# Two fp4 feed-forward stages: when the third group of rows is normalised, scaled and rounded

## The chip, the cores and the metric

The kernel runs on one core of a Trainium2 chip. Its engines are TensorE (PE; its weight loads are shown as PEld), VectorE (DVE), ScalarE (ACT), GpSimd (POOL) and SyncE (SP), which issues most of the transfers. The metric is the time of one execution in device microseconds; 2608.18 us is the median of the three runs before the change (2606.8 to 2610.64). Each profile is of one execution and has a time of its own.

## The reference, cut to what matters

The reference is a chain of six residual blocks on `x`, 8192 rows of 256 numbers (8 x 1024 x 256): an fp4 feed-forward block, an attention with decaying state, the same fp4 block again, a ternary feed-forward block, an attention with memories, the ternary block again. The change touches the two fp4 blocks:

```python
def fp4_quant_dequant(x):            # along the last dim, blocks of 16
    scale = max(|block|) / 6         # at least 1e-12
    idx = searchsorted(_MID, |x / scale|)
    return _GRID[idx] * sign(x) * scale   # grid 0 .5 1 1.5 2 3 4 6
def fp4_linear(x, w):
    return einsum('bsk,nk->bsn', fp4_quant_dequant(x), fp4_quant_dequant(w))

n = layernorm(x)                          # per row of 256
h = silu(fp4_linear(n, w_gate)) * fp4_linear(n, w_up)    # 704 wide
x = x + 0.5 * fp4_linear(h, w_down)
...
x = x + decay_attention(layernorm(x)); then the fp4 block again
```

So a row is normalised, cut into 16 blocks, each divided by its scale and rounded to the fp4 grid; the product goes through the gate and is quantised a second time, in 44 blocks, ahead of the last product.

## The kernel before, in words

All of `x` lies in SBUF as 16 groups (`NG`) of 4 tiles (`G`), a tile being 128 rows. `ffn_fp4` is called twice: `ffn_fp4(True, "decay")` is the first stage, which prepares weights on the way, and `ffn_fp4(False, "ternary")` the second; `attn_decay("fp4")` lies between them. Each call runs a loop over `i`, one pass per tile (64 tiles and a short tail), with `g, j = divmod(i, G)`. A helper `pin` fixes the order of the instructions on each engine to the order in which the code issues them, transfers on SP's queue included.

One pass for tile `i` does this. PE makes the two halves of the gate and the up product (`products`, L835; `pg` has one buffer, `pu` two). ACT takes the silu (`sg`, L846), DVE multiplies (`h`, L848). Between the halves ACT takes the magnitudes of the tile before (L795) and DVE rounds it to a bf16 grid `gd` (`round_grid`, L858, two instructions). After the second half DVE finds the block scales of this tile's `h` (`scale`, L783 to L787), POOL divides by them (L791), and ACT copies the scales (L790) for PE to turn in the next pass (`scales_turned`, L863).

The scales of the tile before go through `spread`: ACT copies them (`sct`, L869), SP writes them to DRAM (`sd`, L871), turns the grid by a transposing transfer (`gt`, L884) and reads the scales back, spread over the partitions, into `ht` (L876). Two passes later POOL multiplies grid and scales (`multiplied`, L899; called by `scaled_turn`), and PE makes the last product one pass after that (`down`, L932), which DVE adds to `x` (L941). In the first stage `down` begins at tile 5.

The rows that later tiles need come the same way. For a group `t` of 2 or more, in halves of two tiles: ACT normalises into `xn` (`ln.normalize`, L317 subtracts the mean, L325 multiplies), DVE and POOL scale it, ACT takes magnitudes (`mgx`) and DVE rounds to a bf16 grid, which lies in the same bytes as the first tile of that half of `xn`. The pass after that SP turns this grid (`gtx`, L1048, one buffer) and the scales, which went with that tile's own through `spread`, come back into `xt` (L876, second call). A pass later POOL multiplies them. There is one `xn` buffer for all groups, so the normalising of the next group into a half must wait for the turn of the grid there.

Before the change the times of these steps follow one rule for every group `t`:

| step | half 0 | half 1 |
|---|---|---|
| normalise | 4t-7 | 4t-5 |
| scale | 4t-6 | 4t-4 |
| round | 4t-5 | 4t-3 |
| turn the grid | 4t-4 | 4t-2 |
| multiply | 4t-3 | 4t-1 |

For the third group (`t` = 2) half 0 is thus normalised in tile 1, scaled in 2, rounded in 3, turned in 4 and multiplied in 5; group `t` = 3 is normalised into half 0 in tile 5. The groups 0 and 1 are made ahead of the loop or by PE's transposes in tile 3.

The statistics come from `statistics(sizes, dues)`: groups are taken together by `sizes`, and each lot is spread evenly over the tiles up to the due tile of its first group. A lot is `bn_stats` and `bn_aggr` on each tile (L235, L236) and then four terms for all its rows at once (L248 to L264: a seed and three Newton steps of a reciprocal square root, on DVE). `ln.advance(i - 1, 1)` issues the terms, in tile `i` ahead of the normalising, and `ln.advance(i, 0)` the tile statistics, at the end of tile `i`. The lots that are due at tile 0 are done before the stage: for the second stage by `begin("fp4", ...)`, which spreads them over 12 passes near the end of `attn_decay`, and ends with normalising group 0.

In the first stage `prepared(i)` adds to the tiles 1 to 4 the quantising of the last weights (`prep_down_scale`, L378 to L384; `prep_down`, L391 to L395), and tile 5 turns them on PE (`prep_down_turn`, L641), two PSUM buffers that ACT empties (`wd`, L645). The load of `raw_w` (L962) then goes on SP's queue.

Of the kernel before, what the change touches and what calls it, by code (L numbers as in the profile page):

```python
# [18 lines left out]
P = 128  # L19
D = 256  # L20
# [19 lines left out]
def macaron_kernel(  # L40
# [227 lines left out]
    def statistics(sizes, dues):  # L268
# [75 lines left out]

    NT = NG * G
    PLANS = {
        "start": ((2, 1, 1, 2, 4, 4, 2), [max(0, G * (g - 2) + 1) for g in range(NG)]),
        "fp4": ((2, 1, 1, 2, 4, 4, 2), [max(0, G * (g - 2) + 1) for g in range(NG)]),

        "decay": ((2, 2, 4, 4, 4), [max(0, G * g - 5) for g in range(NG)]),  # L350
        "ternary": ((2, 2, 4, 4, 4), [max(0, g - 1) for g in range(NG)]),
# [393 lines left out]
    def ffn_fp4(prepare, after):  # L745
        with ExitStack() as st:
# [164 lines left out]
            def turn(i):  # L911
                h, _ = hs.pop(i)
                ht = hp.tile([P, NC, P], F32, tag="ht", name="ht", bufs=HT_BUFS)
                for c0, c1 in ((0, 4), (4, 5), (5, 6)):
                    kn = DCH[c0][1]
                    pa = ps_t.tile([P, 4, P], F32, tag="pt", name="pt")
                    for c in range(c0, c1):
                        k0 = DCH[c][0]
                        pin(
                            nc.tensor.transpose(pa[:kn, c - c0, :], h[:, k0 : k0 + kn], ident)  # L920
                        )
                    pin(nc.scalar.copy(ht[:kn, c0:c1, :], pa[:kn, : c1 - c0, :]))
                hts[i] = (ht, DCH[-1][1])
# [61 lines left out]
            sc1 = fp4_scale(v1, lnp, nc.gpsimd, pin)  # L985
            xts[1] = (xn1,)

            xn = None
            downs = 0

# [3 lines left out]
            for i in range(NT + 3):  # L994
                g, j = divmod(i, G)
                h = hp.tile([P, NI], F32, tag="h", name="h") if i < NT else None

                to = (i + 7) // G
                to_do = to < NG and i > 0
                half = 0 if j in (1, 2, 3) else 1  # L1000
                if i == 0 and not prepare:
                    xts[0], copied = turn_products(xts[0])
                    copied()
                pts = None
                for q in range(2):
                    if i < NT:
                        pg = ps_h.tile([P, NHALF], F32, tag="pg", name="pg", bufs=1)
                        pu = ps_h.tile([P, NHALF], F32, tag="pu", name="pu")
                        products(i, q, 0, pg)
                        if q == 1 and i == 3:  # L1010
                            xts[1], copied = turn_products(xts[1][0])
                        if prepare and late_weights and q == 1:
                            late_weights.pop()(ps_t)
                        if q == 1 and by_dma(i - 1):
                            pts = scales_turned(i - 1)
                        products(i, q, 1, pu)
                        gated(h, q, pg, pu)
                    if q == 0:
                        while copies and i < NT:
                            copies.pop(0)()  # L1020
                    elif i == 3:
                        copied()

                    if 0 < i < NT and q == 0:
                        magnitudes(hs[i - 1][0], qp[:, 0:NI])
                        if by_dma(i - 1):
                            round_grid(hs[i - 1][0], qp[:, 0:NI], gd[:, :NI])
                    if i == NT - 1:
                        if q == 1:
                            round_(*hs[i - 1], qp[:, 0:NI])  # L1030

                        part = h[:, q * NHALF : (q + 1) * NHALF]
                        at = NI + q * NHALF // 8
                        mul = nc.vector if q else nc.gpsimd
                        halves.append((part, scale(part, hp, at, mul)))
                    if i == NT:
                        copies.pop(0)()
                        part, sc = halves.pop(0)
                        mg = ps_h.tile([P, NHALF], F32, tag="pu", name="mg")
                        magnitudes(part, mg)  # L1040
                        round_(part, sc, mg, nc.vector if q else nc.gpsimd)
                if pts is not None:
                    spread(i - 1, pts)
                for to_, half_ in list(xgrids):
                    gx, at = xgrids[to_, half_]
                    if at == i - 1:
                        gt = lnp.tile([P, G, P], BF16, tag="gtx", name="gtx", bufs=1)
                        pin(nc.sync.dma_start_transpose(out=gt, in_=gx))  # L1048
                        xgrids[to_, half_] = (gt, at)
                if i == 0:  # L1050
                    mgs = [qp[:, 0 : 2 * D], ps_t.tile([P, 2 * D], F32, tag="pt", name="mg1")]
                    for n in range(2):
                        magnitudes(v1[:, 2 * D * n : 2 * D * (n + 1)], mgs[n])
                if 0 < i < NT:

                    ln.advance(i - 1, 1)
                if to_do and j % 2 == 1:
                    if j == 1:
                        to_n, tiles = to, (0, 1)
                        if xn is None:  # L1060
                            xn = xn_pool.tile([P, G, D], F32, tag="xn", name="xn")
                    else:
                        to_n, tiles = (i + 5) // G, (2, 3)
                    if to_n < NG:
                        for n in tiles:
                            ln.normalize(xn, to_n, n, pin)
                if by_dma(i - 3):
                    scaled_turn(i - 3)
                if NT - 2 <= i - 2 < NT:
                    turn(i - 2)  # L1070
                for key in list(xgrids):
                    gt, at = xgrids[key]
                    if at == i - 2:
                        xgrids.pop(key)
                        to_m, half_m = key
                        multiplied(xts[to_m][:, G * half_m : G * half_m + G, :], gt)
                if i < NT:
                    own = scales[i % 2] if by_dma(i) else None
                    if own is not None:
                        scale(h, hp, NI, sc=own[:, : NI // 16])  # L1080
                        hs[i] = (h, own)
                    else:
                        hs[i] = (h, scale(h, hp, NI) if i < NT - 1 else None)

                    if j % 2 == 0 and i > 1:
                        to_s, half_s = ((i + 6) // G, 0) if j == 2 else ((i + 4) // G, 1)
                        if 1 < to_s < NG:
                            scale(
                                x_part(half_s), lnp, NI + 88,
                                sc=own[:, NC * 8 : NC * 8 + 2 * D // 16],  # L1090
                            )
                            xhalf[i] = (to_s, half_s)
                    if j % 2 == 1 and i > 1:
                        to_r, half_r = ((i + 5) // G, 0) if j == 3 else ((i + 3) // G, 1)
                        if 1 < to_r < NG:
                            v = x_part(half_r)
                            mg = ps_t.tile([P, 2 * D], F32, tag="pt", name="mgx")
                            magnitudes(v, mg)
                            gx = v.bitcast(BF16)[:, 0 : 2 * D]
                            round_grid(v, mg, gx)  # L1100
                            xgrids[to_r, half_r] = (gx, i)
                    if i == 0:
                        nb = 2 * D // 16
                        for n in range(2):
                            round_(
                                v1[:, 2 * D * n : 2 * D * (n + 1)],
                                sc1[:, nb * n : nb * (n + 1)], mgs[n],
                            )
                    ln.advance(i, 0)
                    if NT - 18 <= i < NT - 2:  # L1110
                        begin(after, NT - 2 - i)
                if prepare and i == DOWN:
                    prep_down_turn(ps_t, "pt")
                if i >= DOWN or not prepare:
                    first = downs
                    while downs <= (i - 4 if i < NT else i - 3) and downs < first + 2:
                        down(downs, *((ps_t, "pt") if downs > first else ()))
                        downs += 1
                if prepare:
                    prepared(i)  # L1120
# [964 lines left out]
```

## Time and profile before

| | us |
|---|---|
| median of the runs | 2608.18 |
| profiled execution | 2604.35 |
| its span | 2602.6 |
| first fp4 stage (34 to 563 of the span) | 529, PE busy 498.22 |
| decay attention (563 to 1004) | 441, PE busy 435.46 |
| second fp4 stage (1004 to 1500) | 496, PE busy 484.29 |
| rest (1500 to 2602) | 1102, PE busy 1080.9 |

The borders between the stages are read off the timeline by eye. In the timeline a line gives the start in microseconds, the duration, the engine (SPq is SP's queue), the line of the kernel, the operation, what it writes and reads, and in square brackets how long the engine stood idle before it and what released it. On the timeline tile 1 of the second stage starts near 1010 and its tile 5 near 1045.

### The profile page before, as it was taken

The numbers are of one execution on the slowest core, as the hardware profiler recorded it, in microseconds if no ns is written. First come the engines' busy times: TensorE is split into PE (matmuls) and PEld (weight loads), VectorE is DVE, ScalarE is ACT, GpSimd is POOL, SyncE is SP. The second block draws the span as 40 slices with busy tenths as digits, with TensorE's granted clock in tenths as the row PEclk, the third lists the DMA queues.
The fourth block names the chain that finished last, engine by engine and source line by source line (L and its number), as shares of the span: only waits on it lengthen the run. The fifth ranks groups of instructions, "written<-read, shape, count | busy, mean of one in ns | idle before, by whom it ended". The sixth has DMA issues, their size and how long they took to land.

```text
span 2602.6 us, 52695 instructions
## 1 busy us (share of the span) xinstructions
PE 2504.2 (96%) x20426; PEld 1864.2 (72%) x20426; DVE 2107.9 (81%) x5040; ACT 1235.8 (47%) x2785; POOL 902.6 (35%) x895
## 2 busy tenths in 40 slices
PE   4899999999999998999999999999999999999999
PEld 2566776766666665677777789995677767678998
DVE  7899999858777678998889789657888888879864
ACT  5344444433433333444444366665555555437664
POOL 4555555521100102555555400004555555540000
PEclk9899999999999999999999999999999999999999
DMA  7455565510000001556555300000000000000001
GB/s 218 99 111 120 119 114 112 110 32 2 2 2 2 2 2 29 113 117 116 115 114 118 81 1 1 1 1 1 2 2 2 2 2 2 2 2 25 33 33 42
DMA packets 197883, 130.32 MB, mean 50 GB/s; under 512 B 137824, under 2 KB 173696, under 8 KB 197632
## 3 DMA queue, kind: packets, MB, share of 16 engines
q1 hardware_dynamic: 196688, 125.75, 22.3%
q8 instruction: 161, 2.64, 0.4%
q0 software_dynamic: 240, 0.54, 0.1%
q14 instruction: 90, 0.74, 0.1%
q10 hardware_dynamic: 704, 0.66, 0.1%
HBM read 78.67 MB, written 16.52 MB: 37 GB/s over the span
## 4 chain that ended last, share of the span: by engine, by line
PE 80%; DVE 11%; ACT 3%; DMA 3%; issue 2%; POOL 1%; SPq 1%; DVEq 0%; POOLq 0%; ACTq 0%
PE po L932 10%; PE po L1207 9%; PE pg L835 9%; PE ph L1180 9%; PE pu L835 8%; PE sc L1250 5%; PE py L1334 5%; PE pq L1348 4%; PE pkv L1348 4%; PE pk L1348 4%; PE po L1348 4%; PE py L1316 2%; PE pmo L1765 2%; DVE at L1259 1%; DMA gtx<-xn 1%
## 5 line engine op out<-in xcount | busy, mean ns | idle before, releaser
L835 PE MATMUL pg<-wgu,xt 128*128 128x352 f32 x1024 | 350.0, 465 | 13.4 <-ACT sg L846 13.1
L932 PE MATMUL po<-wd,ht 128*128 128x256 f32 x1536 | 356.0, 382 | 2.3 <-DVE x L941 1.8
L835 PE MATMUL pu<-wgu,xt 128*128 128x352 f32 x1024 | 348.9, 464 | 2.1 <-DVE h L848 1.9
L932 PEld LDWEIGHTS po<-wd,ht 128*128 128x128 f32 x1536 | 291.7, 191 | 66.0 <-issue 4.1
L791 POOL TENSOR_TENSOR h<-h,q_rs 128x704 f32<-128x704 f32 (+1 forms) x128 | 176.3, 1378 | 419.9 <-DVE q_rs L787 419.9
L846 ACT ACTIVATE sg<-pg 128x352 f32<-128x352 f32 x256 | 117.8, 460 | 399.3 <-PE pg L835 394.0
L835 PEld LDWEIGHTS pg<-wgu,xt 128*128 128x128 f32 x1024 | 194.9, 192 | 108.5 <-ACT sg L846 21.1
L835 PEld LDWEIGHTS pu<-wgu,xt 128*128 128x128 f32 x1024 | 187.1, 193 | 103.3 <-issue 14.7
L1207 PE MATMUL po<-w,hl 128*128 128x256 f32 x1024 | 243.9, 280 | 1.4 <-DVE hl L1191 1.2
L1207 PE MATMUL po<-w,hh 128*128 128x256 f32 x1024 | 243.4, 280 | 0.0
L1881 POOL TENSOR_TENSOR mo<-mo 128x256 f32<-128x256 f32 x192 | 164.3, 856 | 195.0 <-DVE mo L1778 186.5
L899 POOL TENSOR_TENSOR ht<-gt,ht 128x768 f32<-128x768 bf16 x124 | 206.4, 1664 | 0.0
L1180 PE MATMUL ph<-xh,w 128*128 128x512 f32 x512 | 204.4, 401 | 1.4 <-ACT hf L1188 0.6
L1180 PE MATMUL ph<-xl,w 128*128 128x512 f32 x512 | 202.2, 396 | 0.0
L1191 DVE TENSOR_TENSOR hl<-hf,hh 128x512 fp32r<-128x512 f32 x256 | 168.2, 683 | 39.6 <-ACT hh L1189 36.1
L1207 PEld LDWEIGHTS po<-w,hl 128*128 128x128 f32 x1024 | 192.1, 188 | 4.5 <-DVE hl L1191 2.5
L1207 PEld LDWEIGHTS po<-w,hh 128*128 128x128 f32 x1024 | 192.0, 188 | 2.6 <-DVE x L1215 0.3
L848 DVE TENSOR_TENSOR h<-sg,pu 128x352 f32<-128x352 f32 x256 | 131.6, 514 | 60.0 <-PE pu L835 53.1
L1188 ACT ACTIVATE hf<-ph,b1c 128x512 f32<-128x512 f32 x256 | 168.3, 696 | 18.5 <-PE ph L1180 16.1
L1259 DVE TENSOR_TENSOR at<-sc,dec 128x512 f32<-128x512 f32 x256 | 158.5, 681 | 16.6 <-PE sc L1250 16.5
L1259 DVE TENSOR_TENSOR at<-sc,tri 128x512 f32<-128x512 f32 x256 | 164.6, 678 | 0.4 <-PE sc L1250 0.4
L1189 ACT CAST hh<-hf 128x512 fp32r<-128x512 f32 x256 | 149.2, 628 | 17.0 <-PE po L1207 15.2
(276 smaller groups left out, 5304.0 us busy)
## 6 DMA issues: line engine op xcount, KB each, us to landing
ht<-sd SPq DMA_DIRECT2D x124, 384.0 KB
xt<-sd SPq DMA_DIRECT2D x56, 256.0 KB
sd<-sct SPq DMA_DIRECT2D x124, 64.0 KB
x<-in_x SPq DMA_DIRECT2D x15, 512.0 KB
out<-x SPq DMA_DIRECT2D x15, 512.0 KB
raw_w<-in_w_t SPq DMA_DIRECT2D x2, 1024.0 KB
gt<-gd SPq DMA_TRANSPOSE x124
gtx<-xn SPq DMA_TRANSPOSE x56
```

The costliest lines, as they stand in the source:

```text
L791: pin(mul.tensor_tensor(vb, vb, rs[:, :, None].to_broadcast([P, nb, 16]), ALU.mult))
L835: nc.tensor.matmul(ps, lhsT=xts[g][:, 2 * j + k, :], rhs=wgu[:, k, (2 * q + of_up) * NHALF : (2 * q + of_up + 1) * NHALF], start=(k == 0), ...
L899: nc.gpsimd.tensor_tensor(wide.rearrange("p c t -> p (c t)"), grid.rearrange("p c t -> p (c t)"), wide.rearrange("p c t -> p (c t)"), ALU. ...
L932: nc.tensor.matmul(po, lhsT=ht[:kn, c, :], rhs=wd[:kn, c, :], start=(c == 0), stop=(c == NC - 1),)
L1180: nc.tensor.matmul(ph, lhsT=w1[:, k, f * P : (f + 1) * P], rhs=xt[:, k, :], start=(k == 0 and xt is xh), stop=(k == 1 and xt is xl),)
L1188: nc.scalar.activation(hf, ph, AF.Gelu, bias=b1c[:, f : f + 1])
L1189: nc.scalar.copy(hh[:, f, :], hf)
L1191: nc.vector.tensor_tensor(hl[:, f, :], hf, hh[:, f, :].bitcast(F32), ALU.subtract)
L1207: nc.tensor.matmul(po, lhsT=ht[:, f, j * P : (j + 1) * P], rhs=w2[:, f, :], start=(f == 0 and ht is hh), stop=(f == NF - 1 and ht is hl),)
L1259: nc.vector.tensor_tensor(at, sc.rearrange("p m (e t) -> p (m e) t", e=2), weight, ALU.mult)
L1348: nc.tensor.matmul(dst, lhsT=lhsT, rhs=rhs, start=n == 0, stop=n == len(parts) - 1)
L1881: summed = nc.gpsimd.tensor_tensor(mo[:, :, :, 0, :], mo[:, :, :, 0, :], mo[:, :, :, m, :], ALU.add)
```

## The change

In the second stage the statistics and terms of the third group are made before the stage: the lots of the plan `"fp4"` are 3, 1, 2, 4, 4, 2 groups, and the groups 0 to 2 are due at tile 0. In the first stage the lots stay, and the third group's is due at tile 2 instead of 1, so its terms come in tile 2.

In both stages the third group's half 0 takes each step a tile later: normalised in tile 2, scaled in 3, rounded in 4, turned in 5, multiplied in 6. Its half 1 keeps its tiles (normalised 3, scaled 4, rounded 5, turned 6, multiplied 7), and so do all groups from the fourth on; group 3 is normalised into half 0 in tile 5, as before. The tiles are now listed in dictionaries ahead of the loop instead of being worked out in it.

Within a tile the code now issues POOL's multiplications (`scaled_turn`, then `multiplied` for the `xt` half) ahead of SP's turn of the next grid and of ACT's normalising. The one buffer of `gtx` is used by half 0 until tile 6, where half 1's turn is issued.

```diff
     PLANS = {
-        "start": ((2, 1, 1, 2, 4, 4, 2), [max(0, G * (g - 2) + 1) for g in range(NG)]),
-        "fp4": ((2, 1, 1, 2, 4, 4, 2), [max(0, G * (g - 2) + 1) for g in range(NG)]),
+        "start": (
+            (2, 1, 1, 2, 4, 4, 2), [max(0, G * (g - 2) + 1 + (g == 2)) for g in range(NG)]
+        ),
+        "fp4": ((3, 1, 2, 4, 4, 2), [0 if g < 3 else G * (g - 2) + 1 for g in range(NG)]),
...
+            norms, x_scales, x_rounds = {}, {}, {}
+            for t in range(2, NG):
+                n01, s0, n23, r0, s1, r1 = (2, 3, 3, 4, 4, 5)
+                if t > 2:
+                    n01, s0, n23, r0, s1, r1 = (G * t + k for k in (-7, -6, -5, -5, -4, -3))
+                norms[n01, 0], norms[n23, 1] = t, t
+                x_scales[s0], x_scales[s1] = (t, 0), (t, 1)
+                x_rounds[r0], x_rounds[r1] = (t, 0), (t, 1)
...
                 if pts is not None:
                     spread(i - 1, pts)
+                if 0 < i < NT:
+                    ln.advance(i - 1, 1)
+                if by_dma(i - 3):
+                    scaled_turn(i - 3)
+                for key in list(xgrids):
+                    gt, at = xgrids[key]
+                    if at == i - 2:
+                        xgrids.pop(key)
+                        to_m, half_m = key
+                        multiplied(xts[to_m][:, G * half_m : G * half_m + G, :], gt)
                 for to_, half_ in list(xgrids):
                     gx, at = xgrids[to_, half_]
                     if at == i - 1:
                         gt = lnp.tile([P, G, P], BF16, tag="gtx", name="gtx", bufs=1)
                         pin(nc.sync.dma_start_transpose(out=gt, in_=gx))
                         xgrids[to_, half_] = (gt, at)
-                if to_do and j % 2 == 1:
-                    if j == 1:
-                        to_n, tiles = to, (0, 1)
...
-                    else:
-                        to_n, tiles = (i + 5) // G, (2, 3)
-                    if to_n < NG:
-                        for n in tiles:
-                            ln.normalize(xn, to_n, n, pin)
-                if by_dma(i - 3):
-                    scaled_turn(i - 3)
+                for half in range(2):
+                    if (i, half) in norms:
...
+                        for n in (2 * half, 2 * half + 1):
+                            ln.normalize(xn, norms[i, half], n, pin)
...
+                    if i in x_scales:
+                        scale(
+                            x_part(x_scales[i][1]), lnp, NI + 88,
+                            sc=own[:, NC * 8 : NC * 8 + 2 * D // 16],
+                        )
+                        xhalf[i] = x_scales[i]
+                    if i in x_rounds:
+                        v = x_part(x_rounds[i][1])
+                        mg = ps_t.tile([P, 2 * D], F32, tag="pt", name="mgx")
+                        magnitudes(v, mg)
+                        gx = v.bitcast(BF16)[:, 0 : 2 * D]
+                        round_grid(v, mg, gx)
+                        xgrids[x_rounds[i]] = (gx, i)
```

More of the change, by code (lines that the diff above doesn't have):

```diff
@@ L996, in ffn_fp4 @@
                 h = hp.tile([P, NI], F32, tag="h", name="h") if i < NT else None
-                to = (i + 7) // G
-                to_do = to < NG and i > 0
-                half = 0 if j in (1, 2, 3) else 1
                 if i == 0 and not prepare:
@@ L1043, in ffn_fp4 @@
                     spread(i - 1, pts)
+                if i == 0:
+                    mgs = [qp[:, 0 : 2 * D], ps_t.tile([P, 2 * D], F32, tag="pt", name="mg1")]
+                    for n in range(2):
+                        magnitudes(v1[:, 2 * D * n : 2 * D * (n + 1)], mgs[n])
+                if 0 < i < NT:
[8 more added lines that the diff above has]
+                        multiplied(xts[to_m][:, G * half_m : G * half_m + G, :], gt)
                 for to_, half_ in list(xgrids):
@@ L1049, in ffn_fp4 @@
                         xgrids[to_, half_] = (gt, at)
[L1050 to L1056, printed above, removed]
-                if to_do and j % 2 == 1:
-                    if j == 1:
-                        to_n, tiles = to, (0, 1)
+                for half in range(2):
+                    if (i, half) in norms:
                         if xn is None:
                             xn = xn_pool.tile([P, G, D], F32, tag="xn", name="xn")
-                    else:
-                        to_n, tiles = (i + 5) // G, (2, 3)
-                    if to_n < NG:
-                        for n in tiles:
-                            ln.normalize(xn, to_n, n, pin)
-                if by_dma(i - 3):
-                    scaled_turn(i - 3)
+                        for n in (2 * half, 2 * half + 1):
+                            ln.normalize(xn, norms[i, half], n, pin)
                 if NT - 2 <= i - 2 < NT:
                     turn(i - 2)
[L1071 to L1076, printed above, removed]
                 if i < NT:
@@ L1083, in ffn_fp4 @@
                         hs[i] = (h, scale(h, hp, NI) if i < NT - 1 else None)
[L1085 to L1101, printed above, removed]
+                    if i in x_scales:
[11 more added lines that the diff above has]
+                        xgrids[x_rounds[i]] = (gx, i)
                     if i == 0:
```

## The prediction

> **What bounds the kernel now.** I read the page first (engines, chain), then busy time by stretch, then the instructions in order of time around the first tiles of both fp4 stages, the only place that the edit touches.
>
> ```profile
> span 2602.6 us, 52695 instructions
> PE 2504.2 (96%) x20426; PEld 1864.2 (72%) x20426; DVE 2107.9 (81%) x5040; ACT 1235.8 (47%) x2785; POOL 902.6 (35%) x895
> PE 80%; DVE 11%; ACT 3%; DMA 3%; issue 2%; POOL 1%; SPq 1%; DVEq 0%; POOLq 0%; ACTq 0%
> ```
>
> PE is the bound; time is won or lost only where PE stands. By stretch (columns: length, busy us of PE, PEld, DVE, ACT, POOL, granted clock, DMA share, GB/s):
>
> ```profile
> 61.00:100.00 39.00, 27.11 (x98) 17.46 (x97) 31.08 (x73) 14.54 (x36) 20.62 (x18) 0.82 0.45 110
> 563.00:1004.00 441.00, 435.46 (x5870) 301.17 (x5870) 320.06 (x817) 160.01 (x321) 39.23 (x17) 1.00 0.01 2
> 1020.00:1031.00 11.00, 6.34 (x13) 3.68 (x13) 8.23 (x27) 3.74 (x9) 1.39 (x1) 0.69 0.31 77
> 1060.00:1490.00 430.00, 427.29 (x1666) 307.97 (x1664) 377.15 (x850) 178.52 (x451) 232.66 (x170) 1.00 0.55 112
> ```
>
> From tile 7 on, the second fp4 stage leaves PE idle 2.7 of 430 us: a delay put in at its start stays in the span. PE's holes lie in 1020 to 1031 and in 61 to 100. The first of them in order of time (second stage, tiles 1 and 2):
>
> ```profile
> 1018.79 1.45 PE L835 MATMUL pu<-wgu,xt 128*128 128x352 f32 x4 [0.93 <-DVE h L848]
> 1021.27 0.51 ACT L317 ACTIVATE xn<-x,ln_b 128x256 f32<-128x256 f32 x1 [4.78 <-DVE ln_b L255]
> 1023.05 0.51 ACT L325 ACTIVATE xn<-xn,ln_r 128x256 f32<-128x256 f32 x1 [1.28 <-DVE ln_r L264]
> 1024.40 0.44 ACT L846 ACTIVATE sg<-pg 128x352 f32<-128x352 f32 x1
> 1024.90 2.71 PE L835 MATMUL pg<-wgu,xt 128*128 128x352 f32 x4 [4.66 <-ACT sg L846]
> ```
>
> ACT stands at the third group's normalising, which needs terms that DVE makes in the same tile; the silu behind it frees PE's only `pg` buffer. Tile 5 of that stage, with the queue of transfers (SPq):
>
> ```profile
> 1044.17 1.24 SPq L884 DMA_TRANSPOSE gt<-gd  x1
> 1046.25 1.20 SPq L1048 DMA_TRANSPOSE gtx<-xn  x1
> 1051.19 0.51 ACT L317 ACTIVATE xn<-x,ln_b 128x256 f32<-128x256 f32 x1 [0.92 <-DMA gtx<-xn]
> 1051.99 1.23 SPq L884 DMA_TRANSPOSE gt<-gd  x1
> 1053.34 0.62 SPq L876 DMA_DIRECT2D ht<-sd  x1
> 1054.02 0.58 SPq L876 DMA_DIRECT2D xt<-sd  x1
> 1055.06 0.44 ACT L846 ACTIVATE sg<-pg 128x352 f32<-128x352 f32 x1
> ```
>
> The group-3 normalising overwrites the part of `xn` that holds group 2's grid, so it waits for `gtx`. That was issued a tile earlier, and still ACT waited 0.92 us. The same tile of the first stage:
>
> ```profile
> 85.15 0.51 ACT L317 ACTIVATE xn<-x,ln_b 128x256 f32<-128x256 f32 x1 [1.52 <-DMA gtx<-xn]
> 87.87 1.22 SPq L884 DMA_TRANSPOSE gt<-gd  x1
> 90.33 0.36 ACT L645 COPY wd<-ptd 128x256 f32<-128x256 f32 x1
> 90.75 0.69 PE L641 MATMUL ptd<-ident,wd_n 128*128 128x128 f32 x2 [3.98 <-ACT wd L645]
> ```
>
> **The change, part by part.** Against the profiled execution, 2604.35 us (span 2602.6, 1.75 around it); the median of the runs is 2608.18, 3.8 higher.
>
> *Extra statistics in the decay stage.* Four tiles by 0.55 us (`bn_stats` to the next) is 2.2 us of DVE in a stretch where PE is busy 435 of 441 us and DVE 320. They lie beside PE: 0 (bounds 0 to 2.2, if that cover is gone).
>
> *Second stage, tiles 0 to 4.* DVE loses three of the four statistics before tile 1's first `h` (1.6 us) and the 12 term instructions after its second (1020.81 to 1022.99, 2.2 us); ACT loses the stop and the 2 us of normalising there. `pg` of tile 2's second half then goes at 1018.9 rather than 1024.9. What is late next is the round that each tile's scales make: DVE scale (2.4 us from the second `h` to the last reciprocal's end), POOL multiply (1.39), ACT magnitudes (0.76), silu (0.45), then PE, and beside them DVE's rounding (2.1 from the first `h` to the second). Set end to end with these rows: tile 1, first `h` 1016.7, second 1018.8, scale to 1021.2, POOL to 1022.6, ACT to 1023.4, silu, PE begins tile 3 at 1023.9 (was 1029.97): 6.1 us won. Tile 2: rounding from 1023.5, second `h` 1025.2, scale to 1027.6, POOL 1029.0, ACT 1029.8, silu 1030.2, the first `xt` copy 0.55, PE's turn of scales 1030.7 (was 1035.91): 5.2 won. The 2 us of normalising, now in tile 2, lie on ACT while it would wait for POOL. Tile 3 has the scale of `xn` more (1.40 on DVE, 1.06 on POOL, 0.1 on ACT) and the rounding less (0.58 on ACT, 1.35 on DVE): magnitudes at 1036.2 (was 1041.5). Tile 4 has the rounding more: after its second `h` at 1038.7 come terms 1.0, scale 1.84, `xn` scale 1.40, `xn` rounding 1.35 and one addition 0.3, so tile 5's first `h` starts at 1044.9 (was 1048.87), the grid's second pass at 1046.2, and `gt`, 0.95 behind it as in tile 4, is issued at 1047.2 (was 1051.99): 4.8 us won at that point. Bounds 3 (PE idles near half of 1020 to 1024 and could fall to half clock) to 5.4 (tile 4's 1.35 us hidden).
>
> *Second stage, tile 5.* `gtx` of half 0 moves from tile 4's place in SP's queue to the end of tile 5's: behind `sd`, `gt`, `ht` and now `xt` too. Order on ACT is unchanged: the group-3 normalising is in tile 5 still, now for a transfer issued in the same tile. In the trace `gtx` came 7.0 us after its tile's `gt` issue (1044.17 to 1051.19) with `ht` alone between; 78.42 to 85.15 in the first stage was 6.7. `xt` adds 256 KB; at the 115 to 196 GB/s of the slices in which `ht` moved that is 1.3 to 2.2 us. I take 8.6 (bounds 8.0 to 9.2). So it lands at 1055.8; normalising (1.9) and magnitudes of half 1 (0.5) follow, and the silu of tile 6 starts at 1058.2, 3.2 us later than the 1055.06 of before. PE, out of work since 1049.7, waits some 9 us. It then starts at half clock: after the 4.66 us stop its next eight matmuls took 5.07 us for 2.5. Before lost that at 1024.9, tile 2; the change loses it here, behind the earlier win. PE ends tile 6 at about 1066.4, was 1061.3: **+5** (bounds +2 to +8).
>
> [...]
>
> *First stage, tiles 0 to 4.* Here the statistics stay in the stage: the four of tile 0 remain, the terms move to tile 2, and normalising still follows them at once. So ACT's stop moves from tile 1 to tile 2, where it ends at 61.6 by the same steps (silu of tile 3 was at 62.24). PE wins 4.5 us at tile 3's start (56.3 for 60.8), then waits 3.3 us for that silu and loses it again. At tile 4 DVE has the 1.35 us of rounding more, 0.6 of Newton steps less; POOL's turn of tile 2 ends at 86.4 to 87.9 (was 87.84), and `gt` follows it. Won: 0 to 1.5; I take 0.5.
>
> *First stage, tile 5.* `gt` at 87.4, `gtx` 8.6 later at 96.0; normalising and magnitudes 2.4; then ACT's first `wd` copy at 98.4 instead of 90.33. PE's `wd` turns stood waiting for that copy for 3.98 us; they go on 8.1 us later, half clock costs 1 more: **+9** (bounds +6 to +11).
>
> *The rest.* `gtx` of half 1 gets a wait for POOL's multiply of half 0 (one buffer); it is free near 1057 in the second stage and SP asks near 1066: 0. Behind it in SP stand only the next tile's transfers. The 1024 KB `raw_w` load stays behind `gtx`, since it waits for PE's `wd` turns: 0. POOL's `xt` multiply goes from tile 5 to 6, two tiles ahead of its use: 0. Groups 3 on keep their tiles.
>
> Sum: 0 + 5 + 9 = 14 us: 2618 for the profiled execution, **2622 us** beside the median.
>
> **The rivals.** 0.2% (5.2 us) is about what a measurement of this kernel tells from no change.
>
> *The turn overtakes.* If `gtx` did not queue behind `ht` and `xt` it would take about as long as a 64 KB `sd`, first of its tile: 3.09 to 3.64 us in the chain, instead of the 5.9 that 8.6 leaves after its own issue. That is 2.8 us per stage less: +8, 2616. Against it: the `gtx` pieces of the chain, each behind an `ht`, take 4.67 to 5.59. [...] The row (4.94 us from issue to ACT's release) fits a queue; by free passing the sum would be the +8.
>
> [...]
>
> *Faster: tile 5 does not wait.* If the normalising found `gtx` landed, only the wins remain: 4.8 and up to 1.5, 2602. It decides at a landing within about 5.4 us of `gt`'s issue in the second stage (8.6 less 3.2), and even then the first stage's 8 must vanish as well. Against it: 6.7 and 7.0 us with less in the queue.
>
> *Within 0.2%.* Overtaking in both stages together with the largest early wins: 2611.
>
> **How the numbers follow.** Forecast (+9 to +19) 0.63; overtaking 0.12, of which 0.02 falls inside 0.2%; spread clock 0.13; faster 0.07; the mishap of small effects 0.05. So slower 0.86, same 0.07, faster 0.07. The bounds give +8 to +21 before overtaking and clock; leaving out the faster case and the ends of the others, 2613 to 2632.
>
> **What would show it.** In tile 5 of both stages ACT's first normalising waits for `gtx` by 5 us or more, SP shows `ht`, `xt`, `gtx` in one row, PE waits 7 to 10 us for a silu (second stage) and some 12 for a `wd` copy (first), with the half clock after it. In tile 2 of the second stage PE's 4.66 us wait is gone; in the first stage a wait of 3 us appears at tile 3. The forecast is wrong if `gtx` lands within 6 us of `gt`, or if PE takes up the delay in later tiles.

## The result, and the profile after

The changed kernel takes 2621.98 us (median of 6 runs, 2618.96 to 2624.1) against 2608.21 (6 runs, 2606.32 to 2610.64): a ratio of 1.0051, 95% interval 1.0038 to 1.0064, 13.8 us slower. Its profiled execution took 2624.1 us, 19.75 more than that of before: that of before was a short one (3.8 below its median), this one a long one (2.1 above).

Lines in the changed file are 2 higher than before in the region of the feed-forward (the silu is L848, the grid's turn L886, `ht` and `xt` L878, the `wd` copy L647), and `gtx` is L1069. From the page of after, its span, the engines' busy time and two groups (busy time, mean ns of one, then idle time ahead of them and what ended it):

```profile
span 2621.6 us, 52691 instructions
PE 2506.7 (96%) x20426; PEld 1866.6 (71%) x20426; DVE 2107.2 (80%) x5028; ACT 1235.8 (47%) x2785; POOL 902.0 (34%) x895
...
L837 PE MATMUL pg<-wgu,xt 128*128 128x352 f32 x1024 | 348.5, 463 | 16.7 <-ACT sg L848 16.5
...
L317 ACT ACTIVATE xn<-x,ln_b 128x256 f32<-128x256 f32 x248 | 117.9, 504 | 100.1 <-DMA gtx<-xn 85.6
```

No engine has more work: PE is busy 2.5 us longer, DVE 0.7 less (1500 to 1510, 1530 to 1540 and 2350 to 2360 have a granted clock of 0.83; in before no such stretch from 1060 on is below 1.00). What grew is ACT's waiting for `gtx`, 85.6 us against 59.0. Of the growth of 26.6, 21.8 lies in the two waits of tile 5 (13.31 and 10.93 for 1.52 and 0.92). The later one first, in tile 5 of the second stage. The timeline of after (start, duration, engine or queue, operation, and in brackets the idle time and what ended it):

```profile
1034.51 1.45 PE L837 MATMUL pg<-wgu,xt 128*128 128x352 f32 x4 [1.30 <-ACT sg L848]
...
1041.47 0.33 PE L865 MATMUL pts<-ident,sc 128*128 128x128 f32 x1 [2.24 <-ACT xt L826]
...
1058.07 1.25 SPq L886 DMA_TRANSPOSE gt<-gd  x1
1059.43 0.61 SPq L878 DMA_DIRECT2D ht<-sd  x1
1060.09 0.59 SPq L878 DMA_DIRECT2D xt<-sd  x1
1060.73 1.21 SPq L1069 DMA_TRANSPOSE gtx<-xn  x1
1066.76 0.51 ACT L317 ACTIVATE xn<-x,ln_b 128x256 f32<-128x256 f32 x1 [10.93 <-DMA gtx<-xn]
1069.17 0.44 ACT L848 ACTIVATE sg<-pg 128x352 f32<-128x352 f32 x1
1069.66 2.72 PE L837 MATMUL pg<-wgu,xt 128*128 128x352 f32 x4 [8.49 <-ACT sg L848]
1072.38 2.55 PE L837 MATMUL pu<-wgu,xt 128*128 128x352 f32 x4
...
1077.39 1.35 PE L837 MATMUL pg<-wgu,xt 128*128 128x352 f32 x4
```

The second stage begins 10.63 us later than before (its first `pg` at 1016.65 for 1006.02); less that, the rows can be set beside before. Tile 2's stop of 4.66 us is gone and tile 3 begins at 1023.9 (was 1029.97). Then SP shows `ht`, `xt` and `gtx` in one row, ACT stands 10.93 us for the last of them, PE 8.49 us for the silu behind, and its next eight matmuls run at half clock (granted 0.50 from 1066 to 1074; 2.72 and 2.55 us for two rows that take 1.35 each further down). Tile 7 begins at 1066.8, was 1061.30: the win of 6.1 at tile 3 has turned into a loss of 5.5. The first stage, same view:

```profile
56.71 1.45 PE L837 MATMUL pg<-wgu,xt 128*128 128x352 f32 x4 [1.36 <-ACT sg L848]
...
62.75 1.45 PE L837 MATMUL pg<-wgu,xt 128*128 128x352 f32 x4 [3.41 <-ACT sg L848]
...
86.92 1.24 SPq L886 DMA_TRANSPOSE gt<-gd  x1
88.22 0.59 SPq L878 DMA_DIRECT2D ht<-sd  x1
88.86 0.58 SPq L878 DMA_DIRECT2D xt<-sd  x1
89.49 1.20 SPq L1069 DMA_TRANSPOSE gtx<-xn  x1
95.53 0.51 ACT L317 ACTIVATE xn<-x,ln_b 128x256 f32<-128x256 f32 x1 [13.31 <-DMA gtx<-xn]
...
97.94 0.36 ACT L647 COPY wd<-ptd 128x256 f32<-128x256 f32 x1
98.36 0.69 PE L643 MATMUL ptd<-ident,wd_n 128*128 128x128 f32 x2 [12.54 <-ACT wd L647]
...
101.57 7.29 PE L934 MATMUL po<-wd,ht 128*128 128x256 f32 x24
108.69 1.35 PE L837 MATMUL pg<-wgu,xt 128*128 128x352 f32 x4
```

PE's wait for the `wd` copy is 12.54 us where it was 3.98, and tile 6 begins at 108.69, was 99.67; this execution's first `pg` came 0.6 later, so 8.4 us are lost here.

By such starts the spans' 19.0 us of difference split: 0.6 ahead of the first tile, 8.4 to tile 6 of the first stage, 1.6 from there to the second stage, 5.5 to its tile 7, 2.9 after it. The two places where steps were moved hold 13.9, which is what the medians say (13.8). The other 5.1 lie where no step was moved, and the runs of one kernel differ by as much (before ran from 2603.08 to 2613.07 in the experiments). One thing was added there, the statistics in the decay attention, and it cost nothing: from the last `po` of the first stage to the first `pg` of the second it is 442.88 us, before 442.86.

### The profile page after: what moved, and what is told of

Same layout as the page of the kernel before. It is cut to its first block, busy times and chain, and to the rows that moved or that the text cites. A ratio compares the mean times of both kernels' runs of the same rounds, so it can differ in the third digit from the quotient of the medians.

```text
span 2621.6 us, 52691 instructions
## 1 busy us (share of the span) xinstructions
PE 2506.7 (96%) x20426; PEld 1866.6 (71%) x20426; DVE 2107.2 (80%) x5028; ACT 1235.8 (47%) x2785; POOL 902.0 (34%) x895
## 4 chain that ended last, share of the span: by engine, by line
PE 81%; DVE 11%; ACT 3%; DMA 2%; issue 2%; POOL 1%; SPq 0%; ACTq 0%; DVEq 0%; POOLq 0%
PE po L934 10%; PE po L1205 9%; PE pg L837 9%; PE ph L1178 9%; PE pu L837 8%; PE sc L1248 5%; PE py L1332 5%; PE pq L1346 4%; PE pkv L1346 4%; PE po L1346 4%; PE pk L1346 4%; PE py L1314 2%; PE pmo L1763 2%; DMA gtx<-xn 2%; DVE at L1257 1%
## 5 line engine op out<-in xcount | busy, mean ns | idle before, releaser
L848 ACT ACTIVATE sg<-pg 128x352 f32<-128x352 f32 x256 | 117.8, 460 | 397.4 <-PE pg L837 388.5
L317 ACT ACTIVATE xn<-x,ln_b 128x256 f32<-128x256 f32 x248 | 117.9, 504 | 100.1 <-DMA gtx<-xn 85.6
```

## The experiments

Kernels of one set were timed beside the kernel before on the same chip: 2608.11 us for the first four, 2607.67 for the next four, 2608.19 for the last two.

### Without the wait

The third group's first half is rounded into a tile of its own, so that no normalising has to wait for its turn by `gtx`. Nothing else of the change is touched.

```diff
                     if i in x_rounds:
                         v = x_part(x_rounds[i][1])
                         ...
                         gx = v.bitcast(BF16)[:, 0 : 2 * D]
+                        if x_rounds[i] == (2, 0):
+                            gx = lnp.tile([P, 2 * D], BF16, tag="own", name="own", bufs=1)
```

> The changed kernel, but the third group's half 0 is rounded into a tile of its own instead of into the bytes of xn, so the normalising of group 3 in tile 5 overwrites nothing that the turn still reads; order and steps stay. Theory (the wait for gtx in tile 5 of both stages is the whole loss): ACT's waits of 10.9 and 13.3 us for gtx are gone, the second stage keeps its early win of about 5 us, the first comes out within 1 us of before: 2602, 6 us below before. Rival (the moved scaling and rounding on DVE or the half clock lose the time by themselves): it stays above before, 2612 to 2622.

Measured: 2600.51 us, ratio 0.9973 (0.9962 to 0.9983). Tile 5 of both stages, PE's rows in its timeline:

```profile
90.65 0.69 PE L643 MATMUL ptd<-ident,wd_n 128*128 128x128 f32 x2 [4.59 <-ACT wd L647]
...
1049.58 1.45 PE L837 MATMUL pg<-wgu,xt 128*128 128x352 f32 x4 [0.79 <-ACT sg L848]
...
1055.32 1.35 PE L837 MATMUL pg<-wgu,xt 128*128 128x352 f32 x4
```

The 12.54 us are 4.59, the 8.49 are 0.79, with 1.45 us for the row behind where it was 2.72, and the kernel is 21.5 us faster than the changed one, 7.6 faster than before. So the whole loss is the normalising's wait for `gtx`, and it hid a win; what is left is the early win (tile 7 of the second stage starts 51.06 us after its first `pg`, before 55.28).

### The statistics alone

The kernel before with the plan `"fp4"` of the change and nothing else.

```diff
-        "fp4": ((2, 1, 1, 2, 4, 4, 2), [max(0, G * (g - 2) + 1) for g in range(NG)]),
+        "fp4": ((3, 1, 2, 4, 4, 2), [0 if g < 3 else G * (g - 2) + 1 for g in range(NG)]),
```

> The kernel before with one part of the change alone: the second stage's third group has its statistics and terms made ahead of the stage; no step moves. Theory: the first stage is as before; in the second, PE's wait of 4.66 us and its slow restart in tile 2 shrink to under 2 us, gtx stays a tile ahead of its use, so the win is kept: 4 to 6 us faster, 2603. Rival (the four more statistics in the decay stage cost their 2.2 us, or a later wait takes the win): 2606 to 2610.

Measured: 2602.07 us, ratio 0.9977 (0.9968 to 0.9987): 6.0 us faster. Its second stage:

```profile
1022.66 1.45 PE L835 MATMUL pg<-wgu,xt 128*128 128x352 f32 x4 [1.29 <-ACT sg L846]
...
1049.26 1.45 PE L835 MATMUL pg<-wgu,xt 128*128 128x352 f32 x4 [0.43 <-ACT sg L846]
...
1055.00 1.35 PE L835 MATMUL pg<-wgu,xt 128*128 128x352 f32 x4
```

The stop in tile 2 is gone as in the change; `gtx` keeps its place and tile 5 waits 0.43. The early statistics win by themselves; moving the steps a tile later loses it.

### One stage at a time

The change in the second stage only (plan `"start"` as before, and in the first stage the third group follows the rule of all groups), and in the first stage only (plan `"fp4"` as before).

```diff
-                if t > 2:
+                if t > 2 or prepare:
```

```diff
-                if t > 2:
+                if t > 2 or not prepare:
```

> The change in the second stage alone: the first stage keeps its timetable and its due time. Theory: 5 us slower than before (2613): early win 5, loss at tile 5 about 10. Rival (the loss is of the first stage alone): 3 to 5 us faster than before.

> The change in the first stage alone: the second keeps timetable and plan. Theory: 9 us slower than before (2617), with PE's wait of some 12 us for the wd copy in tile 5. Rival (most of the 14 us lies in the second stage): less than 5 us slower.

Measured: second stage alone 2611.2 us, ratio 1.001 (1.0001 to 1.0019), +3.1 us; first stage alone 2616.68, ratio 1.0031 (1.002 to 1.0043), +8.6. Together 11.7, the whole 13.8. The first stage's size is as forecast. The second's is 1.9 below the forecast's 5, which its interval (0.3 to 5.0) just takes in, while its own trace loses 5.8 us between the stage's first `pg` and tile 7; a size between 3 and 6 is as far as this can be told.

### The place in the queue

The changed kernel, with `gtx` of the third group's first half issued ahead of all of tile 5's transfers:

```diff
+                for to_, half_ in list(xgrids):
+                    gx, at = xgrids[to_, half_]
+                    if at == i - 1 and (to_, half_) == (2, 0):
+                        gt = lnp.tile([P, G, P], BF16, tag="gtx", name="gtx", bufs=1)
+                        pin(nc.sync.dma_start_transpose(out=gt, in_=gx))
+                        xgrids[to_, half_] = (gt, at)
                 if pts is not None:
                     spread(i - 1, pts)
```

and with the same issue, as a function `turn_x`, behind `ht` and ahead of `xt` alone:

```diff
                 wide(ht, 0, NC)
                 spreading[i] = ht
+                if xgrids.get((2, 0), (None, None))[1] == i:
+                    turn_x((2, 0))
                 if i in xhalf:
                     ...
                     wide(xts[to][:, G * half : G * half + G, :], NC, NC + G)
```

> The changed kernel with one thing undone: the turn of the third group's first half (gtx of tile 5) is issued ahead of that tile's sd, gt, ht and xt, as in the kernel before, and not behind them. Order on the other engines, statistics and normalising are as changed. Theory (the loss is the place in SP's queue): the grid is rounded in tile 4, so gtx lands about 5 us after its own issue, before ACT has come to the normalising of tile 5 or within 1 to 3 us of it; PE's waits of 8.5 us (second stage) and 12.5 us (first stage) shrink below 2 and 5 us, the half clock after them is gone, and only the early wins remain: 2602 to 2607, median 2605. Rival (the loss is the later rounding, a tile closer to its reader, and the queue adds little): the waits shrink by 2.8 us each at the most, 2616.

> The changed kernel with gtx of the third group's first half issued ahead of xt alone: behind sd, gt and ht of tile 5 as before, but without the 256 KB of xt in front of it. Theory (the queue moves in order, and xt's transfer was priced at 1.3 to 2.2 us of the 8.6): gtx lands 6.4 to 7.3 us after that tile's gt issue, ACT goes on 1.3 to 2.2 us earlier in each stage, PE still waits long enough to fall to half clock: 2.6 to 4.4 us less than the changed kernel, 2618. Rival (the transfer passes what stands ahead of it, so that its landing is set by its own latency from its issue): one issue of 0.6 us less ahead, 1.2 us less in all, 2621.

Measured: ahead of everything 2603.65 us, ratio 0.9982 (0.9973 to 0.9991); ahead of `xt` alone 2617.3, ratio 1.0037 (1.0024 to 1.005). The first is within its theory's range (2602 to 2607); the second is 0.7 us below its 2618, and the rival's 2621 is outside the interval by little, so the trace has to tell. The turn and what waits for it, in the second stage of the first of them:

```profile
1048.72 1.21 SPq L1052 DMA_TRANSPOSE gtx<-xn  x1
...
1051.55 0.51 ACT L317 ACTIVATE xn<-x,ln_b 128x256 f32<-128x256 f32 x1 [2.53 <-DMA gtx<-xn]
```

and in both stages of the second:

```profile
90.28 1.20 SPq L904 DMA_TRANSPOSE gtx<-xn  x1
91.53 0.59 SPq L878 DMA_DIRECT2D xt<-sd  x1
...
95.23 0.51 ACT L317 ACTIVATE xn<-x,ln_b 128x256 f32<-128x256 f32 x1 [11.59 <-DMA gtx<-xn]
...
1055.13 1.21 SPq L904 DMA_TRANSPOSE gtx<-xn  x1
...
1059.83 0.51 ACT L317 ACTIVATE xn<-x,ln_b 128x256 f32<-128x256 f32 x1 [8.97 <-DMA gtx<-xn]
```

From its issue until ACT goes on, the same transfer takes 2.83 us with none of its tile's transfers ahead of it, 4.95 and 4.70 behind `sd`, `gt` and `ht`, 6.04 and 6.03 behind `xt` too (from 89.49 and 1060.73 in the changed kernel). So what stands ahead of it does delay it, though the issue itself takes the same 1.2 us in all three. Whether it waits for the others to end or shares the DMA engines with them, these rows do not tell. In the first stage, with `gtx` issued first, ACT no longer waits for it there but 4.52 us for DVE's terms of the next group, and PE 4.73 us for the `wd` copy, where it was 3.98 before.

### Own tiles for every group

If waiting for `gtx` is what costs, a tile of its own for every grid should help all groups. The edit is in the rounding of `xn`, with two buffers:

```diff
-                        gx = v.bitcast(BF16)[:, 0 : 2 * D]
+                        gx = lnp.tile([P, 2 * D], BF16, tag="own", name="own", bufs=2)
```

It was put into the changed kernel, then into the changed kernel with the first stage's plan of before (terms in tile 1, normalising in tile 2):

```diff
-        "start": (
-            (2, 1, 1, 2, 4, 4, 2), [max(0, G * (g - 2) + 1 + (g == 2)) for g in range(NG)]
-        ),
+        "start": ((2, 1, 1, 2, 4, 4, 2), [max(0, G * (g - 2) + 1) for g in range(NG)]),
```

> The changed kernel with every group's grid rounded into a tile of its own (two buffers), so that no normalising overwrites what a gtx reads. ACT's waits for gtx, 85.6 us in all in the changed kernel and 58.8 us when only the third group's first half has its own tile, are gone everywhere. Theory (of these waits only the two of tile 5 reach PE; in all later groups the silu behind them still comes in time, PE's waits for a silu there are 0.4 us a group): 0 to 4 us less than with the third group's tile alone (2600.5): 2599. Rival (the later waits also cost PE, half of the remaining 58.8 us): 2575.

> The same with own grid tiles everywhere, and the first stage's third-group statistics ended in tile 1, as in the kernel before, while their normalising stays in tile 2, as changed. Theory (ACT's stop, which the change moved from tile 1 to tile 2 of the first stage, goes away only if terms and normalising are a tile apart): PE's 3.41 us wait at tile 3 of the first stage goes, 2.2 us of term work on DVE comes ahead of tile 1's scale; 1 to 3.4 us less than with own tiles alone: 2597. Rival (the first stage is bound by the loads behind it, POOL's copies and the turns of wd, so what is won at tile 3 is lost by tile 5): the same as with own tiles alone, 2599.

then into the kernel before, alone and with the plan `"fp4"` of the change:

> The kernel before, with its own timetable, and every group's grid rounded into a tile of its own (two buffers). ACT's 59.0 us of waiting for gtx go. Theory A (the own tiles are worth about the same 5 us that they brought on top of the third group's in the changed kernel, whatever the timetable): 2603. Theory B (in the timetable of before, gtx is waited for by 0.9 to 1.5 us in tile 5 and PE by 0.4 us behind it, so that there is nothing to win before the later groups, and little there): 2607.

> The kernel before with the third group's statistics made ahead of the second stage, as in the change, its normalising and rounding in the tiles of before, and own grid tiles for all groups. Theory A (parts add up: 5.5 us for the statistics alone, some 5 for the own tiles): 2597. Theory B (own tiles are worth nothing in the timetable of before): 2602. Against the 2593.7 of own tiles with the changed timetable and tile 1's terms it tells whether the later normalising and rounding bring anything of their own: if this kernel is not more than 1 us slower, they bring nothing.

| own tiles in | us | ratio to before, 95% interval |
|---|---|---|
| the changed kernel | 2595.39 | 0.9955 (0.9943 to 0.9968) |
| the same, terms in tile 1 | 2593.66 | 0.9951 (0.9939 to 0.9964) |
| the kernel before | 2599.02 | 0.9967 (0.9954 to 0.9979) |
| before with the early statistics | 2597.82 | 0.9955 (0.9941 to 0.9969) |

In the changed kernel the own tiles won 3.6 us more than the first theory gave them, and its rival's 2575 is far off; in the kernel before they won 4.0 more, and the second theory there falls. PE's waits between 125 and 566 us, the first stage behind its start (us in total, times, longest), in the kernel before:

```profile
PE pts L863 <- ACT sc L790: 6.8, 7, 2.1
PE pg L835 <- ACT sg L846: 1.6, 3, 1.2
```

and with its grids in own tiles:

```profile
PE pts L863 <- ACT sc L790: 4.4, 6, 1.6
...
PE pg L835 <- ACT sg L846: 0.4, 1, 0.4
```

So the later groups' waits for `gtx` did reach PE, 3.6 us in this stretch, mostly by the copy of the scales that stands behind the normalising on ACT. All twelve traces agree on the place: from tile 6 of the first stage to its last `po` the four kernels with own tiles take 458.3 to 460.4 us, the eight others 461.5 to 465.8, and in the second stage, from tile 7 on, there is no such gap (441.8 to 443.2 against 441.8 to 443.5). The profile before had the sign of it: its chain passes seven times through `gtx` between 108 and 513 us, 4.67 to 5.59 us each, and not once in the second stage. Of the 9.2 us won in the medians the rest was not located.

The terms in tile 1 bring 1.7 us, which the intervals do not separate from nothing: the wait of 3.41 us for the silu is gone from that trace, but PE now waits 3.32 us for the scales a little earlier. Whether the parts add is open: the early statistics are worth 6.0 us alone and 1.2 in the medians beside own tiles, while the traces of those two kernels are 4.8 apart at tile 7 of the second stage (54.89 and 50.05 us from its first `pg`). The fastest kernel keeps the change's later normalising, takes its terms a tile earlier and has own tiles: 14.0 us faster than before, 28 than the changed kernel. That the later steps bring anything of their own is not shown: its median is 4.2 us below that of the early statistics with own tiles and the tiles of before, more than the 1 us set beforehand, but the two were timed in different sets and their intervals overlap. In their traces the later steps are 1.8 us ahead at tile 6 of the first stage (63.19 and 65.03 us from its first `pg`) and 1.0 behind at tile 7 of the second (51.05 and 50.05).

## Why the prediction was right

*What bounds tile 5.* The step that decides, `gtx` 8.6 us behind its tile's `gt`, measured 8.61 and 8.69. The price of `xt` in it, 1.3 to 2.2 us, was 1.72 and 1.96 (6.89 and 6.73 from `gt` to ACT without it). It was put down to the bytes alone; 0.63 of it is that `gtx` is issued later, and 1.09 and 1.33 that it lands later after its issue. Taking `xt` out of the way left 9.6 us of the 13.8.

*Second stage.* Forecast against measured, moved by the stage's start: tile 3 at 1023.9, measured 1023.9; the turn of scales 1030.7, 1030.8; `gt` issued 1047.2, 1047.4; PE through with tile 6 at 1066.4, 1066.8. So +5 was +5.5 in the trace; the stage changed alone gave 3.1 in the medians. None of it is taken up later: from tile 7 to the stage's last `po` it is 442.5 us, before 441.8.

*First stage.* Won at tile 3: 56.3 forecast, 56.1 measured (less 0.6); the wait there 3.3, measured 3.41. `gt` came at 86.3, not 87.4: 1.1 us more was won ahead of tile 5 than put down. So the `wd` copy is 7.0 us later instead of 8.1, and the half clock after it (granted 0.50 from 98 to 104 us, before from 90 to 94) cost 1.4 instead of 1 (from the copy to tile 6 10.75 us, before 9.34): +8.4 for +9. That 1 was the author's estimate; the 2.5 of a slow restart in the second stage, read off the 5.07 us of before, came again (5.27 us for 2.7).

*The rest.* Nothing that was costed at 0 shows up: `gtx` of half 1 follows its `ht` at once (1076.66 and 1077.35). The extra statistics, bounded by 2.2 us, cost nothing either. What the spans differ by beyond the two stages' starts is missing in the medians, so it is not put down to the change.

*What was luck.* That the sum met the median to a fraction of a microsecond: the two stages missed by +0.5 and -0.6 in the trace and cancel, and by the medians they add up to 11.7 apart. The two stages, their order of size and the path through `gtx` were not luck; they were read off rows of before.

*The rivals.* "The turn overtakes" falls by the queue experiments, and with it "Within 0.2%". "Tile 5 does not wait" gave 2602 as its price; with the wait taken away it is 2600.5, so the price was right and the condition not met. The 0.13 for a spread clock and the 2632 that ends the range stand for 10 us on top from further slow restarts after short idles of PE; that sum was the author's estimate, and no run shows it. In the profiled execution the granted clock was 1.00 from 36 to 70 us, with the 3.41 us wait at tile 3 in it, and again from 1016 to 1056. The last section shows that the same wait in other kernels did lower it, for up to 1.9 us.

## What to carry to other kernels

When a step is moved a tile later, look for the buffer that its late end holds: here the grid lay in bytes that the next group's normalising overwrites, and that normalising stood ahead of the silu that PE waits for. Here the transfer's price was its place in the queue (2.83 us in front, 6.04 at the end), so a moved issue is costed behind everything that is now ahead of it; one small buffer took the whole loss away. Split a change before judging it: the one line of early statistics was worth 6 us by itself, and the moved steps hid it.

## What the runs showed of the hardware

*The same wait, three clocks.* At tile 3 of the first stage PE waits exactly 3.41 us in six of these kernels, whose first stages are the same up to there. The windows view around the end of that wait (stretch, length, PE busy, granted clock, DMA share, GB/s), for the changed kernel:

```profile
62.00:64.00 2.00, 1.25 (x4) 1.00 0.51 158
64.00:66.00 2.00, 1.16 (x10) 1.00 0.09 26
```

for the changed kernel with all own tiles, where the wait ended at 60.36:

```profile
60.00:62.00 2.00, 1.64 (x6) 0.93 0.39 103
62.00:64.00 2.00, 1.97 (x9) 0.50 0.00 0
64.00:66.00 2.00, 2.00 (x7) 0.72 0.15 37
```

and for the one with `gtx` issued first, where it ended at 61.52:

```profile
60.00:62.00 2.00, 0.48 (x1) 0.65 0.52 163
62.00:64.00 2.00, 2.00 (x4) 0.50 0.10 29
64.00:66.00 2.00, 2.00 (x10) 0.50 0.01 4
66.00:68.00 2.00, 2.00 (x6) 0.65 0.01 2
```

In three of the six the clock stays at 1.00, in one it falls after PE has been running for over a microsecond, in two before PE restarts. From this `pg` to the next it takes 4.52, 5.28 and 6.39 us: in these executions the same wait cost 0 to 1.9 us.

The rows also give the times of the change, as an estimate that takes the clock to step between 1.00 and 0.50. With own tiles it falls at 61.72 (0.93 means 0.28 us at half before 62) and is back at 65.12, 3.4 us later; with `gtx` first it falls at 60.6 and is back at 67.4, 6.8 us later, twice as long. With own tiles PE had been back at work for 1.36 us when the clock fell, and with `gtx` first it had stood for only 2.5 us of its 3.41. What sets the moment of a fall, and how long it lasts, these runs do not show. After each of the waits of 4.66 us and more for a silu (up to 8.97, with the second stage alone changed) the first four matmuls took 2.71 or 2.72 us, against 1.45 in the three kernels whose clock stayed at 1.00 over the 3.41; in the traces of before and after the granted clock at those restarts was 0.50.
